# Routing-list writes handed out tile by tile in a fused cross-attention and mixture-of-experts kernel

## The chip, the cores and the metric

The kernel runs on one core of one Trainium2 chip. The metric is device time in microseconds (us), the median of repeated runs. All engines of the core run their own instruction streams and wait for one another through semaphores: TensorE (PE in the profile, its weight loads PEld), VectorE (DVE), ScalarE (ACT), GpSimd (POOL) and SyncE (SP), which only issues transfers here. A profiled execution gives the times of single instructions.

## The reference

Four sequences of 1024 tokens with 256 features go through two gated blocks, all in float32:

```python
x = x + tanh(g_xattn[0]) * xattn(layernorm(x), ctx, ctx)   # 16 heads of 64, 64 context tokens per sequence
x = x + tanh(g_ffn[0])  * moe(layernorm(x))                # 8 experts, 256 -> 1024 -> 256, silu

# xattn: softmax(qh kh^T) vh, multiplied by qh, projected, plus bias
# moe:   logits = xt gate_w^T; the best 2 of 8 experts of each token, softmax over the two;
#        sum over the two of weight * (silu(xt w1[e]) w2[e])
```

The attention is dense and its work is known ahead. Which tokens go to which expert is known only when the second layer norm of a sequence and its gate scores are done.

## The kernel before, in words

**Groups, tiles, steps.** The 4096 tokens are 8 groups of 512, each of 4 tiles of 128. The main loop runs over `g` from 0 to 10 and, inside, over `t` from 0 to 3; one pass of the inner loop is called a step here. For `g` below 8 a step computes the probabilities of one tile (`probabilities`, L381: scores on TensorE, largest and sum on VectorE, exponential on ScalarE, the multiply by the reciprocal sum on GpSimd, L404). The products with the values, the projection and the residual follow one group later, the second layer norm (`norm_again`) and the gate scores two groups later.

**Routing.** Two groups are one sequence, and a sequence is one batch of routing. In the step `g` = 3, 5, 7 or 9 with `t` = 2, `route` ranks the experts of its 8 tiles; at `t` = 3 `placing` computes, for each token and each of its two choices, the row of a list in DRAM and the entry (token number, weight). `enter` (L562 and on) writes them: for one tile and one choice an indirect DMA on GpSimd (L568) puts 128 entries of 8 bytes into rows of `lists`. That is 16 list writes per batch, 64 in all. Before the change `entries` hands them out in three parts: tiles 0 to 2 at `t` = 3 of that group, tiles 3 to 5 at `t` = 0 of the next, tiles 6 and 7 at `t` = 1, so 6, 6 and 4 writes.

**The planner.** The program is written in an order, and a scheduler sets the order on each engine from it: earlier work has precedence, and later work that its forecast finds ready may go ahead. `behind_softmax` (L837) adds an order on GpSimd: what is issued under it comes after the newest multiply of the probabilities (`newest`, set in `probabilities`). Once the last tile of the attention has had its multiply, `newest` stays what it is.

**Slots.** The experts' work is cut into slots, most of them of 256 list rows of one expert. Slots 0 to 8 take the lists of the first two batches alone and can begin while the attention of the later groups still runs; slots from 9 on need all four. `run_slots` is a generator, and `pieces` says how often each step calls it. Its first piece issues, on SP's queue, the loads of the token numbers of four slots (`load_ids`, L812) and the weights of three (`load_weights`, L830 and L833); its second piece issues the gathers of three slots' normalised tokens on GpSimd (`gather_tokens`, L845); the third transposes the first slot's tokens on TensorE (`transposed`, L867). From then on each slot is: hidden products (`hidden`, L899) with silu on ScalarE (L907), output products (`combine`, L978), a weighting on VectorE (L966), a gather of the output rows (L922), an addition (L970) and a scatter (L939) on GpSimd. Token numbers are loaded four slots ahead, weights and tokens three. The loads of SP's queue are kept in their written order (`behind_loads`). A load of token numbers waits for every list write of the batches that it needs (`apart`, with `lists0` for the first two batches and `lists1` for the others).

**Tables.** `tabling` (L1069 and on) computes on VectorE which expert and rows each slot has: `early_table` after the second batch, `late_table` after the fourth.

## Time and profile before

| | |
|---|---|
| median of 3 runs | 890.65 us (889.99 to 891.10) |
| the profiled execution | 918.12 us |
| its span, first to last instruction | 916.3 us |
| granted TensorE clock, mean over the span | 0.986 |
| TensorE busy | 871.4 us, 95% of the span |
| GpSimd busy | 403.0 us, 44% |
| VectorE busy | 327.8 us, 36% |
| ScalarE busy | 263.9 us, 29% |
| list writes (L568) | 64, 62.1 us in all |

The page gives busy time by engine, the chain of work that ended last, and groups of like instructions with what ended the idle time before them. Times in the lines of a profile are microseconds from the first instruction, and single durations that are marked as a mean are nanoseconds. A line such as `out<-in` names what an instruction writes and reads. In the attention, up to about 400 us, TensorE alternates among queries, scores, transposes and projections; from 350 us on slots' work comes between, and from about 512 us it is slots alone.

### The profile page before, as it was taken

What the parts mean: (1) busy time and instruction counts of PE and PEld (TensorE: products, weight loads), DVE (VectorE), ACT (ScalarE), POOL (GpSimd) and SP (SyncE); (2) the same over time, 40 slices, a digit from 0 to 9 for tenths busy, and PEclk for the clock granted to TensorE, in tenths of its full rate; (3) what the DMA queues carried; (4) which work ended last, traced back from release to release, by engine and by line L of the source; (5) the groups of instructions that cost most, each with busy time, mean ns of one, the idle gap of its engine ahead of it and who ended that gap; (6) DMA issues with size and microseconds to landing.
All of it is one profiled execution on the core that took longest, in us unless ns stands there. A gap on an engine that the chain in (4) does not pass through costs nothing.

```text
span 916.3 us, 11723 instructions
## 1 busy us (share of the span) xinstructions
PE 871.4 (95%) x4328; PEld 657.5 (72%) x4328; DVE 327.8 (36%) x729; ACT 263.9 (29%) x414; POOL 403.0 (44%) x392
## 2 busy tenths in 40 slices
PE   8999999999999998997997899999999999999995
PEld 5556858574857576865885787777777777888884
DVE  3467585777468748631155300000000001100010
ACT  4653353425242425432140121211211211121110
POOL 2051212146213553065447565555455555564443
PEclk9999999999999999998998899999999999999998
DMA  9600000001010225276372575744444564457111
GB/s 203 195 1 1 24 24 24 24 19 30 1 46 1 47 90 188 72 141 143 115 262 63 143 248 166 237 149 140 148 140 142 176 198 148 135 188 267 51 36 42
DMA packets 85279, 102.33 MB, mean 112 GB/s; under 512 B 29366, under 2 KB 71740, under 8 KB 85216
## 3 DMA queue, kind: packets, MB, share of 16 engines
q1 hardware_dynamic: 62656, 66.96, 24.4%
q0 software_dynamic: 11600, 25.25, 8.8%
q10 hardware_dynamic: 10960, 9.31, 3.7%
q8 instruction: 36, 0.59, 0.3%
q14 instruction: 27, 0.22, 0.1%
HBM read 84.75 MB, written 17.33 MB: 111 GB/s over the span
## 4 chain that ended last, share of the span: by engine, by line
PE 80%; DVE 10%; another core or an unknown queue 3%; issue 3%; DMA 1%; POOL 1%; ACT 1%; POOLq 0%; ACTq 0%; DVEq 0%
PE py L978 23%; PE ph L899 22%; PE pp L445 11%; PE pq L370 10%; PE sc L385 5%; PE pa L414 2%; PE pt L867 2%; PE po L428 2%; DVE qT L437 1%; PE pk L317 1%; DVE sm L401 1%; DVE pr L396 1%; DVE mx L394 1%; PE pt_b L281 1%
## 5 line engine op out<-in xcount | busy, mean ns | idle before, releaser
L978 PE MATMUL py<-w,hT 128*128 128x256 f32 (+1 forms) x1168 | 238.3, 369 | 9.2 <-issue 8.7
L899 PE MATMUL ph<-xT,w 128*128 128x256 f32 (+2 forms) x896 | 233.8, 418 | 2.1 <-ACT xT L872 1.2
L978 PEld LDWEIGHTS py<-w,hT 128*128 128x128 f32 (+1 forms) x1168 | 199.8, 184 | 40.2 <-issue 14.0
L899 PEld LDWEIGHTS ph<-xT,w 128*128 128x128 f32 x896 | 170.0, 191 | 57.5 <-issue 1.6
L907 ACT ACTIVATE hT<-ph 128x1024 f32<-128x1024 f32 (+3 forms) x84 | 69.9, 835 | 370.6 <-PE ph L899 319.5
L966 DVE TENSOR_SCALAR x<-py,ids 128x256 f32<-128x256 f32 (+1 forms) x72 | 33.5, 465 | 381.9 <-PE py L978 348.3
L404 POOL TENSOR_TENSOR pr<-pr,sm 128x1024 f32<-128x1024 f32 x32 | 60.9, 1902 | 218.1 <-DVE sm L402 202.1
L370 PE MATMUL pq<-nT_a,wq 128*128 128x512 f32 x256 | 117.0, 597 | 0.4 <-issue 0.2
L445 PE MATMUL pp<-wp,qT 128*128 128x256 f32 x512 | 113.2, 379 | 0.0
L445 PEld LDWEIGHTS pp<-wp,qT 128*128 128x128 f32 x512 | 97.0, 190 | 18.2 <-issue 5.3
L922 POOL DMA_INDIRECT x<-out_dram,ids x68 | 69.3, 1018 | 81.7 <-DMA out_dram<-x,ids 61.9
L845 POOL DMA_INDIRECT x<-normed,ids x68 | 67.9, 999 | 53.4 <-DMA ids<-lists 34.3
L970 POOL TENSOR_TENSOR x<-x,x 128x256 f32<-128x256 f32 (+1 forms) x67 | 48.3, 721 | 90.5 <-DVE x L966 77.8
L370 PEld LDWEIGHTS pq<-nT_a,wq 128*128 128x128 f32 x256 | 45.9, 190 | 53.5 <-issue 47.6
L939 POOL DMA_INDIRECT out_dram<-x,ids x68 | 69.0, 1015 | 23.2 <-POOL x L970 18.0
L568 POOL DMA_INDIRECT lists<-entry,to_row x64 | 62.1, 971 | 20.5 <-issue 17.9
L385 PEld LDWEIGHTS sc<-keys,qT 128*128 128x128 f32 x512 | 62.9, 192 | 7.9 <-issue 7.5
L385 PE MATMUL sc<-keys,qT 128*128 128x128 f32 x512 | 67.4, 278 | 0.0
L415 ACT COPY aT<-pa 128x512 f32<-128x512 f32 x64 | 34.6, 590 | 91.2 <-PE pa L414 71.1
L394 DVE TENSOR_REDUCE mx<-sc 128x16 f32<-128x1024 f32 x32 | 39.0, 1220 | 29.5 <-PE sc L385 28.3
L401 DVE TENSOR_REDUCE sm<-pr 128x16 f32<-128x1024 f32 x32 | 38.9, 1215 | 20.9 <-ACT pr L399 20.9
L377 ACT COPY qT<-pq 128x512 f32<-128x512 f32 x64 | 35.7, 582 | 28.4 <-PE pq L370 28.4
(209 smaller groups left out, 624.8 us busy)
## 6 DMA issues: line engine op xcount, KB each, us to landing
w<-in_L_ffn_w_dram SPq DMA_DIRECT2D x56, 1024.0 KB
out_dram<-x ACTq DMA_DIRECT2D x8, 512.0 KB
normed<-keep_b ACTq DMA_DIRECT2D x8, 512.0 KB
x<-in_x_dram SPq DMA_DIRECT2D x7, 512.0 KB
x<-normed,ids POOLq DMA_INDIRECT x68
x<-out_dram,ids POOLq DMA_INDIRECT x68
out_dram<-x,ids POOLq DMA_INDIRECT x68
wq<-in_L_xattn_w_qs_dram SPq DMA_DIRECT2D x4, 256.0 KB
```

The lines of the kernel that those rows point to most:

```text
L370: nc.tensor.matmul(pq, wq[:, c, p * P : (p + 1) * P], nT[g][:, c, :], start=(c == 0), stop=(c == NC - 1),)
L385: nc.tensor.matmul(sc[:, p // 2, :, p % 2, :], of_pair(qT, p)[:, t * P : (t + 1) * P], kT[g // GB][:, p, :], start=True, stop=True,)
L404: nc.gpsimd.tensor_tensor(pr, pr, sm.unsqueeze(2).to_broadcast([P, H, M]), ALU.mult).ins
L445: nc.tensor.matmul(pp[:, i, :], of_pair(qT, p)[:, t * P : (t + 1) * P], wp[:, p, :], start=(p == 0), stop=(p == NP - 1),)
L568: nc.gpsimd.indirect_dma_start(out=lists, out_offset=bass.IndirectOffsetOnAxis(ap=to_row[:, k, i : i + 1], axis=0), in_=entry[:, k, i, :], ...
L845: gather = nc.gpsimd.indirect_dma_start(out=xin[t][:n], out_offset=None, in_=normed[: tokens_of(s)], in_offset=bass.IndirectOffsetOnAxis(a ...
L899: nc.tensor.matmul(ph[:, i, :], a[:, c, f * P : (f + 1) * P], xT[:, c, :], start=(c == 0), stop=(c == NC - 1),)
L907: nc.scalar.activation(hT[f0 // per_tile][:, f1 : f1 + step, :], ph, AF.Silu)
L922: gather = nc.gpsimd.indirect_dma_start(out=acc[t][:r], out_offset=None, in_=outf[:n], in_offset=bass.IndirectOffsetOnAxis(ap=ids[:r, t, 0 ...
L939: put = nc.gpsimd.indirect_dma_start(out=outf[:n], out_offset=bass.IndirectOffsetOnAxis(ap=ids[:r, t, 0:1], axis=0), in_=acc[t][:r], in_of ...
L970: nc.gpsimd.tensor_tensor(acc[t][:r], acc[t][:r], y[t][:r], ALU.add)
L978: nc.tensor.matmul(py[t][rows], hT[f // per_tile][:, f % per_tile, t * P : t * P + r], b[:, f, columns], start=(f == 0), stop=(f == NF - 1),)
```

## The change

The tiles of a batch are put into a queue, `to_enter`, at `t` = 3, when the batch has been placed. Every step of the main loop then takes from its front: one tile (2 writes) where the batch is the first or third, two tiles (4 writes) where it is the second or fourth. The first and third batch are thus handed out over eight steps, the second and fourth over four, which end one step later than before (`t` = 2 of groups 6 and 10 in place of `t` = 1). Since the first piece of `run_slots` must stand behind the last write of the second batch, the first two pieces move one step on, from `t` = 1 and 2 of group 6 to `t` = 2 and 3. The late table keeps its place.

```diff
-    def entries(g, part):
+    to_enter = []
+
+    def entries():
         nonlocal entered
-        tiles = range(R)[3 * part : 3 * (part + 1)]
-        with behind_softmax():
-            enter(list(range(g - GB + 1, g + 1)), second["places"], tiles)
-        entered += len(tiles)
+        for _ in range(2 if to_enter and to_enter[0][0][0] // GB % 2 else 1):
+            if to_enter:
+                groups, places, tile = to_enter.pop(0)
+                with behind_softmax():
+                    enter(groups, places, [tile])
+                entered += 1
...
     pieces = {
-        HG + 2: (0, 1, 1, 0), HG + 3: (3, 3, 2, 2), HG + 4: (3, 3, 3, 3), HG + 5: (1, 1, 2, 1), HG + 6: (1, 1),
+        HG + 2: (0, 0, 1, 1), HG + 3: (3, 3, 2, 2), HG + 4: (3, 3, 3, 3), HG + 5: (1, 1, 2, 1), HG + 6: (1, 1, 0, 0),
     }
...
             if ends and t == 3:
-                entries(before_last, 0)
-            elif g >= GB + 2 and before_last % GB == 0 and t < 2:
-                entries(before_last - 1, t + 1)
-                if t == 0:
-                    tabling(before_last - 1)
+                groups = list(range(before_last - GB + 1, before_last + 1))
+                to_enter.extend((groups, second["places"], i) for i in range(R))
+            entries()
+            if g >= GB + 2 and before_last % GB == 0 and t == 0:
+                tabling(before_last - 1)
```

Here `HG` is 4, `GB` is 2 and `R`, the tiles of a batch, is 8.

## The prediction

> **What bounds the kernel now.** I read the page first, then the stretches of the span, the chain of waits, GpSimd's groups in the attention, and last the timeline around the first slot. The page says where the time is:

> ```profile
> span 916.3 us, 11723 instructions
> PE 871.4 (95%) x4328; PEld 657.5 (72%) x4328; DVE 327.8 (36%) x729; ACT 263.9 (29%) x414; POOL 403.0 (44%) x392
> ...
> PE 80%; DVE 10%; another core or an unknown queue 3%; issue 3%; DMA 1%; POOL 1%; ACT 1%; POOLq 0%; ACTq 0%; DVEq 0%
> ```

> TensorE is busy for 95% and carries 80% of the chain that ended last; GpSimd (POOL), on which the list writes stand, carries 1%. An edit on GpSimd changes the time only where TensorE is made to wait, or is freed from a wait.

> The profiled execution took 918.12 us, 27.5 more than the median of the runs, 890.65. The busy time by stretch shows where much of that must lie (columns: TensorE, its weight loads, VectorE, ScalarE, GpSimd, granted clock, DMA share, GB/s):

> ```profile
> 406.00:422.00 16.00, 8.00 (x48) 3.07 (x52) 5.62 (x9) 0.71 (x2) 10.55 (x11) 0.91 0.86 117
> 422.00:432.00 10.00, 9.97 (x53) 7.81 (x50) 0.48 (x2) 3.80 (x5) 3.46 (x4) 0.80 0.26 94
> 480.00:492.00 12.00, 11.83 (x57) 10.28 (x57) 8.49 (x40) 0.00 (x0) 9.44 (x10) 1.00 0.40 98
> 492.00:512.00 20.00, 10.96 (x25) 6.41 (x25) 10.77 (x44) 2.52 (x3) 13.24 (x15) 0.66 0.24 43
> ```

> In the first stretch TensorE loses 16.00 - 8.00 = 8.0 us, and after it about 2.0 to a clock of 0.80 (10 x 0.20). In the last one it issues 25 matmuls; at the spacing of a hidden matmul, 6.91 us for 32, those are 5.4 us of work, so 14.6 are lost. With 0.2 from the third stretch the sum is 24.8 us, of the 27.5. In both, TensorE, VectorE and ScalarE stand still together for much of the time, while GpSimd issues list writes without a break, and the chain of waits names nothing that this core's instructions could have held:

> ```profile
> 403.77 17.40 another core or an unknown queue
> ```

> I take both stretches as belonging to the profiled execution: 918.12 - 24.8 = 893.3 is already within 0.3% of the median. So the sixteen-write bursts of the third and fourth batch, ugly as they look, leave little for the ordinary runs to win, at most a few us.

> In the attention GpSimd's multiply of the probabilities (L404) is what a burst could delay. Over the stretch 196 to 350 us, where the first 32 writes are, its idle time was ended by VectorE alone:

> ```profile
> L568 POOL DMA_INDIRECT lists<-entry,to_row x32 | 31.2, 974 | 8.9 <-issue 8.9
> L404 POOL TENSOR_TENSOR pr<-pr,sm 128x1024 f32<-128x1024 f32 x13 | 24.7, 1899 | 69.7 <-DVE sm L402 69.7
> ```

> A burst of six takes 5 x 1.27 + 0.97 = 7.3 us, and a step is about 12, so the burst is over before the next multiply is wanted. (One multiply, at 221.9, came 0.15 us late behind a burst.)

> [...] a list write holds GpSimd for 0.97 us and the next follows 0.30 later. [...] the step from a second token gather to its landing is 2.8 us at the quiet end of the kernel and 5.8 beside the first weight loads. [...]

> **The change part by part.** Counts stay: 64 writes, 16 gathers and loads of the two moved pieces, all other work. Only places in the order change.

> *Writes of the first batch* (two per step instead of 6, 6, 4): gain at most the 0.15 us above. Their lists are wanted only at the first slot, over 100 us later. *Writes of the second batch* (four per step instead of 6, 6, 4): no multiply was late there; they gain nothing themselves, but end one step later.

> *The first two pieces, one step later.* They issue four loads of token numbers, six weight loads of 1 MB (SP) and six token gathers (GpSimd). The timeline before:

> ```profile
> 325.98 0.96 POOL L568 DMA_INDIRECT lists<-entry,to_row  x1 [0.31 <-issue]
> 332.35 3.91 SPq L812 DMA_DIRECT2D ids<-lists  x4
> 333.25 1.90 POOL L404 TENSOR_TENSOR pr<-pr,sm 128x1024 f32<-128x1024 f32 x1 [6.31 <-DVE sm L402]
> 335.30 1.08 POOL L845 DMA_INDIRECT x<-normed,ids  x1 [0.16 <-DMA ids<-lists]
> 337.32 0.10 SPq L830 DMA_DIRECT2D w<-in_L_ffn_w_dram  x1
> 345.73 1.90 POOL L404 TENSOR_TENSOR pr<-pr,sm 128x1024 f32<-128x1024 f32 x1 [2.83 <-DVE sm L402]
> 350.60 0.60 PE L867 MATMUL pt<-ident,x 128*128 128x128 f32 x4
> 355.94 3.72 PE L899 MATMUL ph<-xT,w 128*128 128x256 f32 x16 [1.17 <-ACT xT L872]
> ```

> The loads of token numbers follow the last write by 332.35 - 325.98 = 6.4 us: they wait for it to land. In the changed order the last four writes stand behind the multiply of the step's third tile, which ends at 333.25 + 1.90 = 335.15. Four writes at 1.28 put the last at 335.3 + 3.8 = 339.1, the token numbers at 339.1 + 6.4 = 345.5 and the first weight load, 4.97 behind them as before, at 350.5. The gathers go behind the fourth multiply, which ends at 347.63: the first gather at 347.8, or at 348.5 if it needs the 2.95 us that lay between token numbers and gather before. The first slot's second gather starts 1.3 later, at 349.1 to 349.8, and lands 2.8 to 5.8 later: 351.9 to 355.6. All six end by 355.6 to 356.3, ahead of the next multiply at 357.60.

> TensorE wanted these tokens at 350.60. If its order stays, it waits 1.3 to 5.0 us; behind the transposes lie 3.74 us of scores, so the first hidden matmul comes at 351.9 + 0.43 + 3.74 = 356.1 to 359.8 in place of 355.94: a loss of 0.1 to 3.8, since 1.17 us were idle there anyway. If the scheduler puts the two score tiles ahead of the transposes, these fall at 354.3 to 355.6 and the matmul at 355.7 to 357.0: 0 to 1.1 lost. The first weight, 1 MB behind token numbers and gathers, took at least 4.6 us from issue to landing before (the last of its landing events that the trace holds), so it lands at about 355.1, later beside the gathers, perhaps 357.5: up to 1.5 lost. I take 1.0 us for all this, keep -0.5 (an order that saves part of the 1.17) and +4 as ends. What is next in line is safe: the second slot's hidden matmuls start at 381.79, and the six gathers and four of the weight loads are done 15 us before; the third slot's weights wait for attention's own buffers until 373.77 in any case.

> *Third and fourth batch.* The last multiply of a softmax is at 394.77, and nothing paces writes behind it. Only their rank against slot work changes: two gathers of old output rows (L922 at 414.39) may pass up to eight more writes, 10 us earlier, but TensorE waits for none of these. So I expect both bursts to stay nearly whole. The fourth batch's lists feed token numbers of the tenth slot, and SP has the ninth slot's weights queued behind them. Last write at 503.1, + 6.4 = 509.5, + 4.97 = 514.5 to the weight's issue and about 5.2 to landing, 519.7; the ninth slot's hidden matmuls, 541.4 in this execution, are at 526.8 without the 14.6 lost. That is 7.1 us of cover. Two additions and two scatters may now go ahead of the last four writes, 2 x (0.72 + 1.02 + 0.58) = 4.6 us: hidden, at nothing. If the cover were gone, each us more would be a us of TensorE.

> Sum: -0.15 + 1.0 = +0.85, on the profiled execution's own frame; carried to the median, 890.65 + 0.85 = **891.5 us**. 0.2% is 1.8 us, about what a measurement of this kernel can tell from no change.

> **The rivals.**

> 1. *Hidden* (45%): as summed, 889.0 to 892.4. For it: GpSimd's 1% of the chain. Against it: a scheduler orders each engine by its own forecast, so a late token may shuffle more than I follow.

> 2. *The first slot's tokens and weights come late* (28%), slower: TensorE stands in order at the transposes behind gathers that only start at 347.8. It decides from a hidden start at 357.7 on (355.94 + 1.8). At its upper end, 3.8 plus part of the weight's 1.5, it gives 890.65 + 4.5 = 895; a typical time is 893.5. Against it: TensorE's order has score tiles to put in between.

> 3. *The bursts cost ordinary runs too* (27%), faster: if the two stretches are not wholly the profiled execution's, breaking up the third batch into twos frees TensorE. The unexplained rest between 893.3 and 890.65 points the other way, so I give it a tenth to a fifth of 24.8, 2.5 to 5: 886 to 888. The same case takes in a luckier order of the attention, where TensorE idles 112.0 - 106.3 = 5.7 us in the stretches 196 to 232, 296 to 330 and 330 to 372.

> **How the numbers follow.** Likeliest is the hidden case: 891.5, its own range 889.0 to 892.4. To leave out no more than 2 in 10 I go down to the middle of the third case, 886.5, and up to 895.0, the upper end of the second. Faster 0.27, same 0.45, slower 0.28.

> **What would show it.** After the change: two list writes behind each multiply from 200 to 290 us and four in the next four steps; token numbers near 345.5, gathers near 347.8, the first hidden matmuls at 356 to 358 with a wait before the transposes or before them; GpSimd's multiply still ended by VectorE; the writes of the last two batches still without long gaps; and, if I read the profile rightly, stretches without owner beside them again. Wrong would be: a median that falls by more than 2 us, a first hidden matmul past 360, or TensorE waiting for weights at the ninth slot.

## The result, and the profile after

The changed kernel takes 895.86 us (median of 9 runs, 892.96 to 899.02), the kernel before 890.06 beside it (9 runs, 888.68 to 891.41): a ratio of 1.0058, 95% interval 1.0039 to 1.0077. A second measurement, on another chip, gave 895.17 against 889.43, 1.0064 (1.0050 to 1.0077). The change costs some 5.8 us. The prediction, 891.5 with a range to 895.0, was too low. On three of the six chips that served the runs below, the kernel before itself took 916 to 924 us with a scatter of 10 us and more; executions like these, and the first profile of the kernel before, are called disturbed here, and ratios from there are told, but differences under 1% can't be read from them.

The profiled execution of the changed kernel took 893.92 us. Head of its page, and its chain of waits by engine:

```profile
span 892.2 us, 11720 instructions
PE 861.5 (97%) x4328; PEld 654.5 (73%) x4328; DVE 328.0 (37%) x729; ACT 263.8 (30%) x414; POOL 406.1 (46%) x392
...
PE 81%; DVE 10%; DMA 3%; issue 2%; POOL 1%; ACT 1%; POOLq 0%; SPq 0%; ACTq 0%; DVEq 0%
```

DMA has risen from 1% to 3% of the chain (it is 2% in the undisturbed profile of experiment 1), and "another core or an unknown queue" is gone. The four stretches that had held 24.8 us of lost time (columns as before: length, TensorE, its weight loads, VectorE, ScalarE, GpSimd, clock, DMA share, GB/s):

```profile
406.00:422.00 16.00, 16.00 (x103) 10.59 (x102) 5.92 (x11) 3.62 (x5) 11.07 (x12) 1.00 1.04 144
422.00:432.00 10.00, 10.00 (x49) 8.81 (x48) 1.72 (x5) 1.27 (x2) 2.33 (x4) 1.00 1.03 135
480.00:492.00 12.00, 12.00 (x59) 10.58 (x58) 11.42 (x45) 1.50 (x2) 9.56 (x10) 1.00 0.14 30
492.00:512.00 20.00, 20.00 (x98) 17.60 (x98) 2.36 (x6) 4.74 (x6) 13.15 (x15) 1.00 0.29 47
```

TensorE is busy without a gap, at full clock, although the writes of batch 3 still stand in one row from 399.1 to 423.5, broken only by two gathers of output rows. GpSimd's groups over 196 to 350 us look much as before; the multiply L404 is still released by VectorE for nearly all of its idle time:

```profile
L568 POOL DMA_INDIRECT lists<-entry,to_row x32 | 31.5, 986 | 8.0 <-issue 8.0
L404 POOL TENSOR_TENSOR pr<-pr,sm 128x1024 f32<-128x1024 f32 x13 | 24.7, 1899 | 78.9 <-DVE sm L402 73.9 <-PE pq L370 4.9
```

The chain from the last list write to the first weight load, on GpSimd and SP:

```profile
336.78 0.96 POOL L568 DMA_INDIRECT lists<-entry,to_row  x1 [0.30 <-issue]
342.97 3.92 SPq L812 DMA_DIRECT2D ids<-lists  x4
342.25 1.90 POOL L404 TENSOR_TENSOR pr<-pr,sm 128x1024 f32<-128x1024 f32 x1 [4.51 <-DVE sm L402]
345.61 1.07 POOL L845 DMA_INDIRECT x<-normed,ids  x1 [1.45 <-DMA ids<-lists]
347.67 0.37 SPq L830 DMA_DIRECT2D w<-in_L_ffn_w_dram  x1
```

Each stands some 11 us after its place before. Most of that is the step itself, since the gathers now stand behind the multiply that ends at 342.25 + 1.90 = 344.15; the first one then waits another 1.45 us for its token numbers. What is new is on TensorE. Its timeline at the first slot (start, us, line, operation, in brackets the idle time ahead and what ended it):

```profile
348.85 0.27 PE L867 MATMUL pt<-ident,x 128*128 128x128 f32 x1
352.82 0.55 PE L867 MATMUL pt<-ident,x 128*128 128x128 f32 x3 [3.69 <-DMA x<-normed,ids]
353.20 3.74 PE L385 MATMUL sc<-keys,qT 128*128 128x128 f32 x32
356.77 3.62 PE L899 MATMUL ph<-xT,w 128*128 128x256 f32 x16
361.60 1.09 PE L414 MATMUL pa<-ident,pr 128*128 128x128 f32 x8 [1.21 <-POOL pr L404]
```

and the chain of waits that leads to it (start, us, what; the pieces left out are each under 0.5 us):

```profile
336.78 5.92 DMA lists<-entry,to_row
...
344.18 1.85 DMA ids<-lists
...
346.98 5.79 DMA x<-normed,ids
352.82 0.55 PE pt L867 x3
```

The last list write of batch 2 goes out at 336.78 and lands after 5.92 us; the token numbers follow, then the second gather of the first slot, which lands after 5.79; TensorE stands 3.69 us at its transposes, and another 1.21 at the next transposes of probabilities.

### The profile page after: what moved, and what is told of

Read it like the earlier page. It is cut to its first block, busy times and chain, and to the rows that moved or that the text cites. A ratio compares the mean times of both kernels' runs of the same rounds, so it can differ in the third digit from the quotient of the medians.

```text
span 892.2 us, 11720 instructions
## 1 busy us (share of the span) xinstructions
PE 861.5 (97%) x4328; PEld 654.5 (73%) x4328; DVE 328.0 (37%) x729; ACT 263.8 (30%) x414; POOL 406.1 (46%) x392
## 4 chain that ended last, share of the span: by engine, by line
PE 81%; DVE 10%; DMA 3%; issue 2%; POOL 1%; ACT 1%; POOLq 0%; SPq 0%; ACTq 0%; DVEq 0%
PE py L978 24%; PE ph L899 24%; PE pp L445 9%; PE pq L370 9%; PE sc L385 5%; PE po L428 2%; PE pa L414 2%; PE pt L867 2%; DVE qT L437 1%; DVE sm L401 1%; DVE pr L396 1%; DVE mx L394 1%; PE pk L317 1%; PE pt_b L281 1%; DVE keep_b L277 1%
## 5 line engine op out<-in xcount | busy, mean ns | idle before, releaser
L978 PE MATMUL py<-w,hT 128*128 128x256 f32 (+1 forms) x1168 | 232.5, 365 | 0.0
L899 PE MATMUL ph<-xT,w 128*128 128x256 f32 (+2 forms) x896 | 232.3, 416 | 0.0
L899 PEld LDWEIGHTS ph<-xT,w 128*128 128x128 f32 x896 | 169.1, 190 | 54.5 <-issue 1.3
L966 DVE TENSOR_SCALAR x<-py,ids 128x256 f32<-128x256 f32 (+1 forms) x72 | 33.5, 465 | 372.4 <-PE py L978 348.1
L404 POOL TENSOR_TENSOR pr<-pr,sm 128x1024 f32<-128x1024 f32 x32 | 60.9, 1902 | 223.9 <-DVE sm L402 202.9
L922 POOL DMA_INDIRECT x<-out_dram,ids x68 | 69.4, 1020 | 86.1 <-DMA out_dram<-x,ids 64.0
L845 POOL DMA_INDIRECT x<-normed,ids x68 | 68.1, 1001 | 43.3 <-DMA ids<-lists 23.4
L568 POOL DMA_INDIRECT lists<-entry,to_row x64 | 62.8, 982 | 19.0 <-issue 15.8
L394 DVE TENSOR_REDUCE mx<-sc 128x16 f32<-128x1024 f32 x32 | 39.1, 1222 | 32.3 <-PE sc L385 31.9
```

What stands on the lines that cost most here:

```text
L404: nc.gpsimd.tensor_tensor(pr, pr, sm.unsqueeze(2).to_broadcast([P, H, M]), ALU.mult).ins
L568: nc.gpsimd.indirect_dma_start(out=lists, out_offset=bass.IndirectOffsetOnAxis(ap=to_row[:, k, i : i + 1], axis=0), in_=entry[:, k, i, :], ...
L845: gather = nc.gpsimd.indirect_dma_start(out=xin[t][:n], out_offset=None, in_=normed[: tokens_of(s)], in_offset=bass.IndirectOffsetOnAxis(a ...
L899: nc.tensor.matmul(ph[:, i, :], a[:, c, f * P : (f + 1) * P], xT[:, c, :], start=(c == 0), stop=(c == NC - 1),)
L922: gather = nc.gpsimd.indirect_dma_start(out=acc[t][:r], out_offset=None, in_=outf[:n], in_offset=bass.IndirectOffsetOnAxis(ap=ids[:r, t, 0 ...
L978: nc.tensor.matmul(py[t][rows], hT[f // per_tile][:, f % per_tile, t * P : t * P + r], b[:, f, columns], start=(f == 0), stop=(f == NF - 1),)
```

## Experiments

For a common measure I matched TensorE's instructions of each trace with those of a second profile of the kernel before (`before_again`, below); where the order is the same, the shift between two matched instructions is the time lost or won up to there. In undisturbed traces it changes in three places only (us; the sum is the difference of the spans to within 0.3, for `weights_first` 0.6):

```
                 start (to 200)   first slot (347-372)   before batch 4 (462-512)
spread_1_3_4         -1.01               0.01                   0.55
after                -0.94               3.80                   0.93
after_again          -0.89               6.35                   0.63
second_only          -1.13               5.76                   0.56
weights_first        -0.17               6.82                  -0.01
weights_apart_2      -0.44               3.53                   0.04
busy_pe_2            -1.26               2.39                   0.78
```

The start differs from execution to execution. The third column (place numbers, L533, that wait for `prior`) is as large in `second_only`, whose third and fourth batches stand as before, as in the spread forms; so it isn't the spreading, and what sets it stayed open.

**1. The kernel before, profiled again** (no edit).

> The kernel before, profiled a second time. If the two stretches in which TensorE, VectorE and ScalarE stood still together (406 to 422 and 492 to 512 us) belong to that one profiled execution, they are absent here: a span near 889 us, although the writes of batches 3 and 4 stand in the same bursts. If the bursts cause them in a profile, they come back at the same places and the span is again above 910.

890.14 us. Its page and the two stretches:

```profile
span 888.4 us, 11723 instructions
...
406.00:422.00 16.00, 16.00 (x103) 11.19 (x96) 5.43 (x10) 4.88 (x6) 8.50 (x10) 1.00 1.01 167
...
492.00:512.00 20.00, 20.00 (x99) 17.61 (x98) 1.45 (x3) 4.02 (x5) 10.91 (x12) 1.00 0.61 162
```

The same instructions and the same bursts, and no loss: the bursts alone don't make the stretches.

**2. Spreading alone.** Batches 1, 3 and 4 as after the change; batch 2 in 3, 3 and 2 tiles and the pieces in their old steps.

```diff
-        for _ in range(2 if to_enter and to_enter[0][0][0] // GB % 2 else 1):
+        n = 1
+        if to_enter and to_enter[0][0][0] // GB == 1:
+            n = 3
+        elif to_enter and to_enter[0][0][0] // GB == 3:
+            n = 2
+        for _ in range(n):
...
-        HG + 2: (0, 0, 1, 1),
+        HG + 2: (0, 1, 1, 0),
```

> Batches 1, 3 and 4 handed out as after the change; batch 2 in 3, 3 and 2 tiles and the first two pieces in their old steps. Theory (the late tokens of the first slot cost the time, and spreading by itself gains about 1 us in each of batches 1 and 2): TensorE's transposes of the first slot start without a wait, and the median is 888.5 to 889.8, that is 0.3 to 1.5 under the kernel before. Rival A (the spread writes themselves cost, by holding GpSimd or the queues at many places): 893 to 896 as after the change.

889.41 us (13 runs) against 889.43: ratio 0.9998, 0.9989 to 1.0006. No wait at the transposes, as expected, but no gain either. The expected gain of 1 us per batch came from comparing the changed kernel with the first, disturbed profile of before; against the undisturbed one TensorE's shift stays at -1.00 from 200 to 462 us. Rival A falls: on such a chip the spread writes cost nothing and gain nothing.

**3. The second batch alone.** The kernel before, with batch 2 handed out two tiles a step and the pieces a step later.

```diff
-        tiles = range(R)[3 * part : 3 * (part + 1)]
+        n = 2 if g == HG - 1 else 3
+        tiles = range(R)[n * part : n * (part + 1)]
...
-            elif g >= GB + 2 and before_last % GB == 0 and t < 2:
-                entries(before_last - 1, t + 1)
+            elif g >= GB + 2 and before_last % GB == 0:
+                if t < 2 or before_last == HG:
+                    entries(before_last - 1, t + 1)
...
-        HG + 2: (0, 1, 1, 0),
+        HG + 2: (0, 0, 1, 1),
```

> Only batch 2 handed out two tiles a step over four steps, with the first two pieces a step later; batches 1, 3 and 4 stay in bursts as before. Theory (late tokens): the transposes of the first slot wait 3 to 4.5 us, the whole cost of the change is here, and the gain of batch 1's spreading (about 1 us) is missing: median 894 to 898. Rival A (the spread writes of batches 1, 3 and 4 cost): 889 to 891.

894.97 us against 889.43: 1.0055 (1.0041 to 1.0068). The whole cost is here. TensorE, first slot:

```profile
352.56 0.90 PE L867 MATMUL pt<-ident,x 128*128 128x128 f32 x3 [3.67 <-DMA x<-normed,ids]
353.25 5.89 PE L385 MATMUL sc<-keys,qT 128*128 128x128 f32 x32
```

The wait is the changed kernel's, 3.67 us, but the 32 scores behind it took 5.89 us, not 3.74. The same trace by single microseconds (length, TensorE, granted clock, DMA share, GB/s):

```profile
349.00:350.00 1.00, 0.00 (x0) 1.00 0.93 165
...
351.00:352.00 1.00, 0.00 (x0) 0.50 1.05 348
...
356.00:357.00 1.00, 1.00 (x7) 0.50 1.11 368
357.00:358.00 1.00, 1.00 (x8) 0.62 1.07 345
358.00:359.00 1.00, 1.00 (x12) 1.00 1.06 397
```

The clock is halved from about 351 to 357.8, and the scores lose 2.15 us on top of the wait. In the profiled execution of the changed kernel, after a wait of 3.69, it stayed full. The nine runs of that kernel fall into two groups that fit this: 892.96 to 893.92 (4 runs, mean clock 0.995 to 0.997) and 895.86 to 899.02 (5 runs, 0.992 to 0.995). The five of its second measurement, 893.66 to 896.73 at 0.993 to 0.995, show no such gap.

**4. Weights of two slots ahead of the token numbers**, in the changed kernel.

```diff
-        for s in slots[: ahead + 1]:
-            load_next_ids(s)
-        for s in slots[:ahead]:
+        for s in slots[: ahead - 1]:
             load(s)
         yield
+        for s in slots[: ahead + 1]:
+            load_next_ids(s)
+        for s in slots[ahead - 1 : ahead]:
+            load(s)
+        yield
...
-        HG + 2: (0, 0, 1, 1),
+        HG + 2: (0, 1, 1, 1),
```

> The changed kernel, but SP loads the weights of the first two slots one step earlier, ahead of the token numbers, so that no weight load runs beside the first slot's gathers. Theory (late tokens, of whose lateness about 3 us are the second gather's landing beside the weight loads, 5.8 us where a quiet one takes 2.9): the gathers start at about 345.6 as in the changed kernel, the second one lands in 2.9 to 3.7 us, the transposes wait 0.7 to 1.8 us in place of 3.7, and the median is 889 to 891.5. Rival C (what makes the tokens late is the landing of the list writes and the token numbers alone): the wait stays at 3 to 4 us and the median at 893 to 897.

896.89 us against 889.43: 1.0078 (1.0064 to 1.0091). Worse. Wait and median are those of Rival C (3 to 4 us, 893 to 897), but they came about in a way that neither theory had; the collision moved:

```profile
350.38 1.07 POOL L845 DMA_INDIRECT x<-normed,ids  x1 [5.49 <-DMA ids<-lists]
...
353.27 0.48 PE L867 MATMUL pt<-ident,x 128*128 128x128 f32 x1 [3.52 <-DMA x<-normed,ids]
354.59 0.90 PE L867 MATMUL pt<-ident,x 128*128 128x128 f32 x3 [0.84 <-DMA x<-normed,ids]
```

The second slot's second weight load, issued at 340.21, now ran ahead of the token numbers on SP's queue. By their landing events the first token numbers took 5.46 us where they take 1.80 in the changed kernel, and landed 0.16 us behind that load. The gathers, with no load beside them, did land in 2.8 us each, as expected, but started 4.8 us late.

**5. No weight load beside either.** The first slot's weights a step ahead, the second slot's only when the first slot's second gather has landed.

```diff
+        for s in slots[:1]:
+            load(s)
+        yield
         for s in slots[: ahead + 1]:
             load_next_ids(s)
-        for s in slots[:ahead]:
-            load(s)
         yield
         for s in slots[:ahead]:
             gather(s)
+        for s in slots[1:ahead]:
+            load(s)
         yield
...
-        nc.sync.dma_start(a, w1[bass.ds(e, 1)].rearrange("o (c p) f -> p (o c) f", p=P))
+        load = nc.sync.dma_start(a, w1[bass.ds(e, 1)].rearrange("o (c p) f -> p (o c) f", p=P))
+        if s == 1:
+            tc.add_manual_dep(load.ins, first_tokens[0].name, ...)
```

> The changed kernel with the first slot's weights loaded a step earlier, ahead of the token numbers, and the second slot's weights only when the first slot's second gather has landed; so no weight load runs beside the token numbers or beside the first slot's gathers. Theory: gathers start at about 345.6 and 347.0 as in the changed kernel, the second lands after 2.8 us in place of 5.8, TensorE waits 0.8 to 1.2 us in place of 3.7, the clock stays full, and the median is 889.8 to 891.2. If the landing of the second gather beside the weight loads has no part in it: wait 3.5 to 4 us, 893 to 896.

919.79 us on a chip where the kernel before took 916.05; measured again:

> The same kernel as weights_apart, measured beside a kernel before that isn't itself disturbed by long stretches of standing still. In the trace of weights_apart the second gather landed after 3.6 us and TensorE waited 1.72 us, then another 1.56 for the multiply of the next probabilities. Theory: wait 0.8 to 1.8 us, clock full in every execution, and a loss of 1 to 2 us against the kernel before: 890.3 to 891.7. If the landing beside the weight loads has no part: 893 to 896.

893.26 us against 889.22: 1.0041 (1.0027 to 1.0054). A third of the cost is gone. The chain, then TensorE:

```profile
347.57 3.98 DMA x<-normed,ids
...
351.60 0.55 PE L878 MATMUL pt<-ident,x 128*128 128x128 f32 x3 [2.00 <-DMA x<-normed,ids]
351.98 5.36 PE L385 MATMUL sc<-keys,qT 128*128 128x128 f32 x32
```

The second gather lands after 3.98 us in place of 5.79, and the wait falls by as much, from 3.69 to 2.00: about 1.7 us of the wait is the landing beside the weight loads, 2.0 the late start of the gather. The landing still isn't the 2.8 us of a quiet one, for the expectation left out a store that ScalarE's queue issues at this very time, 512 KB of the residual (at 347.65 here; in the changed kernel it is this line):

```profile
347.18 0.38 ACTq L291 DMA_DIRECT2D out_dram<-x  x1
```

By the trace's records of DMA packets the store moves from 348.6 to 350.7, and the second gather, issued at 347.57, has its own packets only from 350.35 on (in the changed kernel the store moves from 348.1 to 350.8, the gather from 350.0). In the kernel before the gather had landed over 8 us before the store. With a landing of 2.8 the wait would have been about 0.8 (an estimate: 2.00 - (3.98 - 2.8)); no run moved the store, so its part isn't shown by experiment.

The expectation of a full clock missed: after only 2.00 us the scores took 5.36. At full clock the stretch would have cost 3.53 - (5.36 - 3.74) = 1.9.

**6. TensorE kept busy.** Three matmuls of 128x512 into the bank of the first slot's transposes, just ahead of them; their result is overwritten.

```diff
             pt = bank(f"pt_{s}")
+            if s == 0:
+                for _ in range(3):
+                    nc.tensor.matmul(pt, ident, wq[:, 0, :512], start=True, stop=True)
```

> The changed kernel with three extra matmuls of 128x512 into the bank of the first slot's transposes, just ahead of these (their result is overwritten). They fill about 1.3 us of TensorE's wait of 3.7 and shift a few scores behind later work. Theory of the clock (the idle wait [...] halves TensorE's clock afterwards in part of the executions): the wait left is 2.4 to 2.7 us, the scores behind it run at 3.7 us for 32 in every execution, the mean clock is 0.995 or more in all, and no execution lies above 894.5; median 892.5 to 894. Without that theory: executions spread from 893 to 897 as with the changed kernel, with clocks from 0.992.

921.00 us against 916.05 on the same chip as the first measurement of experiment 5. Again:

> The same kernel as busy_pe, measured again for the same reason. Theory of the clock: the wait left behind the extra matmuls is 1.1 to 2.7 us, the scores behind it run at full clock, every execution has a mean clock of 0.995 or more and none lies above 894.5; median 892 to 894. Without that theory: executions from 893 to 897, with clocks down to 0.992.

893.56 us against 889.22: 1.0049 (1.0035 to 1.0062), five runs from 891.85 to 894.82, clocks 0.997 to 0.994.

```profile
348.52 2.74 PE L864 MATMUL pt<-wq,ident 128*128 128x512 f32 x6
...
352.43 0.55 PE L871 MATMUL pt<-ident,x 128*128 128x128 f32 x3 [1.06 <-DMA x<-normed,ids]
352.81 2.40 PE L385 MATMUL sc<-keys,qT 128*128 128x128 f32 x20
...
361.16 1.16 PE L385 MATMUL sc<-keys,qT 128*128 128x128 f32 x8
```

The extra matmuls took 2.74 us, not the 1.3 I had expected (the trace shows six instructions for the three), the wait left was 1.06, and the scores ran at full speed: 2.40 us for 20 is 3.74 x 20 / 32. Work that computes nothing, at the place where TensorE would stand, made the kernel no slower than the changed one; its median is 1.6 to 2.3 us lower. But that isn't the clock alone, for the scheduler also put twelve of the 32 scores behind the hidden products, and the wait of 1.21 us at L414 is gone. This trace and the changed kernel's first both ran at full clock, and yet it loses 2.39 where that lost 3.80: 1.4 us of the gain have nothing to do with the clock. One run of five, 894.82 at 0.994, lies above the bound of 894.5. So this experiment doesn't separate the clock from the order. That the halved clock is a second part of the cost rests on the slow scores themselves, here in `second_only` (5.89 us) and `weights_apart_2` (5.36), below in `after_again` (5.36).

**7. The pieces' step alone.** The kernel before with the first two pieces a step later.

```diff
-        HG + 2: (0, 1, 1, 0),
+        HG + 2: (0, 0, 1, 1),
```

> The kernel before with only the first two pieces a step later; all list writes in their old bursts. Theory (the cost sits in the landing of batch 2's last list writes, one step later): token numbers and weight loads go out at about 331.6 and 336 us as before, only the first two gathers move behind the fourth multiply, to about 345.2 and 346.5; with the weight loads over they land in about 3 us, at 349.5, where TensorE wants them at 349.9: no wait, median 889 to 890.5. Rival D (the piece's step itself, by its place in GpSimd's order, is what costs): 893 to 896.

Four measurements, all on disturbed chips: 921.87 against 916.05, 922.16 against 923.76, 924.63 against 923.55, 923.79 against 921.40; ratios 1.0069, 0.9941, 1.0009 and 0.9987, the last expected as follows:

> The same kernel as pieces_late, once more. On the chips with disturbed executions its ratio to the kernel before was 1.0069, 0.9941 and 1.0009, which decides nothing. Theory: wait at the transposes 0 to 0.8 us, median at most 0.15% above the kernel before. Rival D (the gathers' place behind the fourth multiply costs as much as the change): 0.4% to 0.8% above.

The times decide nothing: the four ratios average 1.000. In the traces TensorE loses 1.5 to 1.7 us from 347 to 372 us in all four, less than half of the changed kernel's 3.80. The gathers stand behind the fourth multiply. In the second and third trace TensorE waits 1.4 and 1.0 us at the transposes; in the first and fourth it hardly waits there (0.4 us and less), but VectorE takes the largest of the first scores (L394) only 3.0 and 3.5 us after these began, against 2.0 in the changed kernel's trace, and the next multiply comes late with it. How much of this an undisturbed chip would show stays open, and with it how the cost divides between the late lists and the late step: no run on an undisturbed chip has the one without the other.

**8. Five us later, not eleven.** As experiment 2, but batch 2 in 2, 2 and 4 tiles.

```diff
-            n = 3
+            n = 2 if len(to_enter) > 4 else 4
```

> Batches 1, 3 and 4 as after the change; batch 2 in 2, 2 and 4 tiles over three steps (4, 4 and 8 writes), first two pieces in their old steps. The last write is at about 330.7 us, 5 later than before, lands at about 336.7, the second gather at 341.5 and its landing at 344.5 to 346, where TensorE wants it at 349: theory (a slack of about 10 us ahead of the first slot's transposes, used up only by a whole step): no wait, median 888.8 to 890.2. If every us of lateness of batch 2's lists costs: 892 or more.

Again on disturbed chips: 925.33 against 916.05, 926.48 against 923.55, 924.27 against 921.40; ratios 1.0109, 1.0029 and 1.0048. In the first trace there is no wait and no loss from 347 to 372 us, but TensorE had lost 6.9 us between 232 and 330 us already, which gave the tokens time; in the other two 2.7 and 2.4 us are lost. Not at the first slot's transposes, whose tokens were there in time, but ahead of them:

```profile
351.56 1.09 PE L414 MATMUL pa<-ident,pr 128*128 128x128 f32 x8 [2.22 <-POOL pr L404]
352.49 0.60 PE L867 MATMUL pt<-ident,x 128*128 128x128 f32 x4
```

The six gathers stand ahead of that multiply on GpSimd, and when their token numbers come later they hold it up. Inconclusive on the median; but the theory's "no wait" was too simple. The slack of the tokens holds, and on the way to it a second wait opens.

**9. The slots a step later.** The changed kernel, its third and later pieces moved.

```diff
-        HG + 3: (3, 3, 2, 2),
+        HG + 3: (0, 4, 3, 3),
```

> The changed kernel with the first slot's transposes (the third piece) and what follows them taken up one step later, ten pieces over three steps instead of four. Writes, token numbers and gathers stay where the change puts them. Theory (the change's whole cost is that TensorE wants the first slot's tokens before they have landed): TensorE has a tile of scores and the products with the values to do first and reaches the transposes after about 358, no wait of more than 0.5 us and no halved clock, and the median returns to 888.8 to 890.5. If the cost is elsewhere (spread writes, gathers behind the fourth multiply, late weights of later slots): 892 to 897.

929.56 against 923.76: 1.0120 (1.0060 to 1.0180), and a second time 933.39 against 923.55, 1.0126. No wait at the transposes, but:

```profile
359.98 2.02 PE L385 MATMUL sc<-keys,qT 128*128 128x128 f32 x16 [3.17 <-DVE pr L396]
365.06 1.53 PE L414 MATMUL pa<-ident,pr 128*128 128x128 f32 x8 [3.06 <-POOL pr L404]
```

Without the slot's products between two tiles of scores, TensorE waits for the softmax instead: 5.6 and 7.1 us lost from 347 to 372 us in the two traces, where the changed kernel lost 3.80 to 6.35. A failed remedy, as far as disturbed chips can tell.

**10. The changed kernel once more.**

> The changed kernel itself, once more. On an undisturbed chip, theory: 893 to 897 beside 889 to 890, a ratio of 1.0045 to 1.0075, the whole loss in one place (350 to 365 us) but for about 1 us before the fourth batch is placed. On a chip where the kernel before itself takes over 910 us, the trace should show 1.0 us less lost near 225 us than the kernel before loses there (its writes stand in sixes, these in twos), 3 to 6 us lost at the first slot, and a ratio of 1.000 to 1.006; if handing the third and fourth batch out in smaller parts helped there, the ratio would be under 0.995.

The undisturbed case: 1.0064, as told above, with a wait of 4.56 us, scores of 5.36 and 6.35 us lost at the first slot.

```profile
353.79 0.55 PE L867 MATMUL pt<-ident,x 128*128 128x128 f32 x3 [4.56 <-DMA x<-normed,ids]
354.17 5.36 PE L385 MATMUL sc<-keys,qT 128*128 128x128 f32 x32
```

No version beat both kernels; experiment 2 equals the kernel before.

## Why the prediction was wrong

**What bounds the kernel, and the two stretches: right for the kernel, too narrow for the chip.** That the 24.8 us don't belong to an ordinary execution held (experiment 1). But I expected the stretches again in the profile after, and they weren't there; and on three chips they were in every profiled execution, in whatever form the writes stood: from 404 to 432 us the nine such traces of burst and spread forms (those of experiment 9 aside) lost 9.8 to 16.1 us, from 462 to 512 between 9.5 and 16.1.

**Writes of the first and second batch: right.** "At most 0.15" stands against 0.00 measured over 200 to 330 us. The third rival, bursts that cost ordinary runs too, falls with experiment 2 for chips at 889 us. On the disturbed ones it had a point, a small one: from 219 to 232 us the burst forms lost 1.0 us in every trace, the two-write forms nothing.

**The first two pieces a step later: the step that failed.** Its times were good: token numbers predicted at 345.5, seen at 342.97; the second gather predicted at 349.1 to 349.8, seen at 346.98: both 2.1 to 2.8 us early, because the disturbed profile that I worked on ran 2.4 us behind by then (multiply at 333.25 there, at 330.87 after). Landing predicted from 351.9 to 355.6, seen at 352.8; wait predicted from 1.3 to 5.0, seen 3.69. What failed is the cost that I drew from it: I put this step at 1.0 us, and it cost 3.80 in the profile at full clock and 6.35 in the other one. Three things made 1.0 us out of it.

- I let a second case pull the value down, in which the scheduler puts two tiles of scores ahead of the transposes. It doesn't: TensorE's order is the same, instruction by instruction, before and after.
- I subtracted 1.17 us of idle time ahead of the first hidden matmul as if it were slack. It isn't. The undisturbed profile of the kernel before shows it:

```profile
355.11 3.72 PE L899 MATMUL ph<-xT,w 128*128 128x256 f32 x16 [1.17 <-ACT xT L872]
...
356.76 1.90 POOL L404 TENSOR_TENSOR pr<-pr,sm 128x1024 f32<-128x1024 f32 x1 [11.70 <-DVE sm L402]
...
358.72 1.09 PE L414 MATMUL pa<-ident,pr 128*128 128x128 f32 x8
```

  The two score tiles behind the transposes also feed a softmax, whose multiply ends at 356.76 + 1.90 = 358.66, and TensorE's next transposes begin at 358.72, 0.06 us later; the weight load ahead of them had stood 0.29 us for this multiply. There is no slack. A delay of the scores passes through that second path in full and comes back as the 1.21 us at L414. So 3.69 - 1.17 + 1.21 = 3.73 of the 3.80 lost.
- The clock was left out. My own table had it at 0.80 from 422 to 432 us, behind the first stretch of standing still. I had forecast waits of up to 5.0 us and put the clock at nothing, without a reason. It cost 2.15 us in `second_only`; of the 2.55 between the changed kernel's two profiles (6.35 - 3.80), 1.62 are slower scores and 0.87 a longer wait.

With the wait at 3.8 at full clock and 2 to 3 us more in over half of the executions, 890.06 + 5.8 = 895.86 is the second rival, which I gave 28% and an upper end of 895.0: the mechanism and place right, the size short by the clock.

**The first weight's 1.5 us: not seen.** The hidden matmuls at 356.77 had no wait (in `busy_pe_2`, where they come at 355.64, they stood 0.43 us for their weights); that the loads delay the *gathers* was where they cost, 1.7 us (experiment 5).

**Third and fourth batch, ninth slot: right.** The bursts stayed nearly whole, and TensorE's list of waits names no weights of the experts. One sum is off: the middle of the third rival's 886 to 888 is 887, not the 886.5 of the range; nothing turns on it.

## What to carry to other kernels

Where a chain of write, landing, read and gather ends at an engine that works in order, count its slack at the consumer (here 349.87 wanted, 339.71 landed: 10.2 us) before moving its first link by a step (11.3 us): beyond it every us is paid, and a chain that has moved may meet other traffic. Here the gather was issued 12.3 us later, with the shift of the start taken out, and landed 1.7 us slower, and 12.3 + 1.7 - 10.2 = 3.8. Short of the slack, the engine that issues the gathers may already be holding up other work (2.22 us at L414 in experiment 8). An idle gap behind the late instruction is slack only if nothing else that it feeds is due sooner (here 1.21 us came back at L414). And a wait on TensorE may cost a second time, through the clock: here 1.6 to 2.2 us in four traces with waits of 2.00 to 4.56 us, nothing in one with 3.69.

## What the runs showed of the hardware

```profile
352.00:353.00 1.00, 1.00 (x8) 0.63 0.65 156
353.00:354.00 1.00, 1.00 (x7) 0.50 0.79 123
...
355.00:356.00 1.00, 1.00 (x8) 0.67 1.02 410
```

With a clock of either 1.00 or 0.50, the shares in such lines give the time of its fall and of its rise (352.3 and 355.7 here). For the five traces, beside TensorE's wait at the transposes (us):

```
                   TensorE waits        clock falls   rises    low for
after_again        349.23 to 353.79        354.2      357.6      3.4
second_only        348.89 to 352.56        350.9      357.8      6.8
weights_first      349.75 to 353.27        352.7      359.5      6.8
weights_apart_2    349.60 to 351.60        352.3      355.7      3.4
after              349.13 to 352.82     stays full
```

The fall came 2.1 to 5.0 us after TensorE had stopped, in `after_again` and `weights_apart_2` only when it was at work again. The same wait cost twice in `second_only` (3.67 us) and once in `after` (3.69); what decides this, the traces don't show.

**A small load behind a large one on the same queue** took 5.46 us in place of 1.80 (experiment 4).

**A gather issued just ahead of a store of 512 KB on another queue** had its packets moved only as the store ended: 3.0 us after its issue in the changed kernel, where the gather before it took 1.8 (experiment 5).

**Disturbed chips.** On them VectorE's copy of the gate scores (L475) came 1.0 us later where GpSimd issued four list writes behind one another (near 225 us), not where it issued two; on undisturbed chips the same bursts cost nothing there (VectorE stood idle ahead of it for 2.70 us in the first profile of the kernel before, for 1.73 in `before_again` and in the changed kernel's). The traces of disturbed executions also lack landing records: all sixteen are there for 119 to 138 of the 268 transfers that GpSimd issues (126 in the first profile of the kernel before), in undisturbed traces for 255 to 261 (258 in the changed kernel's). What holds the engines up on these chips, no run shows.
